# Two graph layers on one core: the first part of the row sums one piece sooner, and one addition of the first layer behind it

## The chip, the cores and the metric

The kernel runs on one core of a Trainium2 chip. The core has five engines with an instruction stream of their own: TensorE (PE) multiplies matrices and writes to the banks of PSUM; its weight loads are listed apart as PEld. VectorE (DVE), ScalarE (ACT) and GpSimd (POOL) work on tiles element by element, and SyncE (SP) issues the transfers (DMA). Each engine runs its instructions in the order of its stream; between engines, an instruction waits for a semaphore. The metric is the device time of one execution in microseconds, as the median of several runs.

## The reference

The input `x` holds 64 graphs with 256 nodes and 512 features, the adjacency matrix `adj` is common to all. There are two layers, each behind a layer norm and a ReLU, each added to its input:

```
h = relu(layernorm(x))
x = x + layer0(h, adj)          # graph attention, one head
h = relu(layernorm(x))
x = x + layer1(h, adj)          # masked attention, eight heads of 64
```

Layer 0 multiplies `h` with a weight of 512x256, forms one score per edge from two vectors, masks and normalises the scores, and puts the weighted sum of the neighbours beside the product itself. Layer 1 projects `h` to queries, keys and values (512x512 each), masks the scores with the same adjacency, normalises them over the neighbours, weighs the values and projects the result with a fourth 512x512 matrix. All is in 32-bit floating point.

## The kernel before

**Groups and phases.** The 64 graphs are taken in 32 groups of two. The main loop (line 1178) runs over the groups `g` and within each over its two graphs `b`. In group `g` the attention of layer 1 is done for the two graphs, and beside it, in pieces, the projections of group `g+1` (`project`), layer 0 of group `g+2` (`first_layer`) and the first layer norm of a later group (`first_norm`). Each of these is a Python generator; a call of `next` emits one piece of it into the instruction streams.

**The step strings.** Which piece follows which is written by hand in two strings (line 1176), one per graph. A letter is one piece: `S` the scores of all eight heads, `m` one masking, `u` a projection, `o` an output product of the graph before, `n` a norm, `s` a piece of layer 0, `f` a piece of `fold`, `v` the differences of the values. Group 0 has a string of its own for its first graph (line 1184), and so has the last group.

**Order on the engines.** TensorE is held to the order of emission by `in_order` (line 131): every matmul is made to follow the one emitted before it. The other engines' instructions are placed by a scheduler, which knows their data dependencies and estimated times; `not_sooner` (line 123) pins an instruction behind the last one that the same wrapper (`Remembers`, line 27) issued to its engine. All of the instructions that go through the wrapper appear under line 35 in the profile, and all matmuls under line 137.

**Seven products.** The big matrix products are done as seven half-size products with sums of blocks (a Strassen-Winograd scheme). For layer 0 this is `first_products` (line 636), from group 2 on. It has seven pieces, with two PSUM banks, `first` and `second`. In the order of emission these are product 1, 2, 6, 7, 5, 4 and 3. `first` accumulates products 1, 6, 5 and 3, `second` product 2 and then, in a new bank, 7 and 4. ScalarE copies a bank aside after products 1, 6 and 7 (`kept`). VectorE adds bank and copy into a quarter of `H` after product 2 (`part(0, 0)`), after product 5 (`part(1, 1)`) and after product 4 (`part(1, 0)`). ScalarE copies the last quarter after product 3. As the bank is read after product 5 and written again by product 3, product 3 waits for that addition. After product 4, `score_rows` (line 621) transposes a few columns of `H` and sends them through memory to all partitions, and GpSimd adds `H` to `x` for the residual. In the profile the seven appear as `ph`: product 6 as `ph<-w_more,sums_xn`, 7 and 4 as `ph<-w_more,hT`, 5 as `ph<-w_sb,sums_r`, and 3 as `ph<-w_sb,sums_xn`.

**Row sums.** The normalisation of layer 1 needs the sum of each row of the exponentials `p`. `fold` (line 984) makes it without TensorE, for every group but the last, in six pieces for two quads of four heads:

1. `put(0)` writes the first quad to memory, `fetch(0)` reads it back rearranged, as `parts` (one transfer and four);
2. `put(1)` writes the second quad;
3. GpSimd adds `parts` down in two additions (`add`, line 1009);
4. `sum_up(0)` (line 1013): VectorE transposes `parts` in blocks and reduces it to `compact`; then `fetch(1)` reads the second quad into the same buffer, with four transfers on SP, each pinned to SP's order;
5. the additions for the second quad;
6. `sum_up(1)` and a reciprocal, which `weigh` (line 1038) uses.

The buffer of `parts` of the first graph is also that of layer 0's edge scores `e`.

In the first string the seven pieces of layer 0 stand in `sssosfsfss`: the pieces of products 1, 2 and 6, an output product, product 7, piece 3 of `fold`, product 5, piece 4 of `fold`, and products 4 and 3.

Of the kernel before, what the change touches and what calls it, by code (L numbers as in the profile page):

```python
# [41 lines left out]
def two_gnn_layers(tc, *args):  # L42

    nc = tc.nc
    with tc.tile_pool(name="verdict", bufs=1) as pool:
        wrong = pool.tile([1, 1], I32, name="wrong")
        bounded(tc, *args, wrong)  # L50
        again = nc.values_load(wrong[0:1, 0:1], min_val=0, max_val=1)
        with tc.If(again > 0):
            tc.strict_bb_all_engine_barrier()
            any_inputs(tc, *args)
# [3 lines left out]
def bounded(  # L58
# [24 lines left out]
    vector, scalar, gpsimd, sync = (  # L83
        Remembers(e) for e in (nc.vector, nc.scalar, nc.gpsimd, nc.sync)
    )
# [23 lines left out]
    def mm(name):  # L109
        return psum.tile([P, 512], F32, tag="turn", name=name, bufs=5)  # L110
# [4 lines left out]
    def after(instruction, name):  # L115

        tc.add_manual_dep(
            instruction.ins, name,
            mybir.DependencyInfo(mybir.DependencyClass.NoSync, mybir.DependencyReason.DATA),
            reason="the engine's order",  # L120
        )

    def not_sooner(engine, operation, *args, **kwargs):

        last = engine.last
        after(getattr(engine, operation)(*args, **kwargs), last)
# [9 lines left out]
    def matmul(*args, **kwargs):  # L136
        in_order(nc.tensor.matmul(*args, **kwargs))  # L137
# [483 lines left out]
    def score_rows(g):  # L621
        rows = small.tile([P, GT, 8], F32, tag="rows", name=f"rows_{g}", bufs=2)
        last = vector.last
        turned = vector.transpose(rows.rearrange("p t c -> p (t c)"), H[:, :, 0:8])
        for other in [last, *fold_last] if g >= 2 else [last]:
            after(turned, other)
        line = dram.tile([P // 8, S], F32, tag="line", name=f"line_{g}")
        not_sooner(sync, "dma_start", line, rows.rearrange("p t c -> p (t c)")[::8, :])
        own = att.tile([P, P // S, GT, S], F32, tag="r", name=f"own_{g}", bufs=1)
        not_sooner(  # L630
            sync, "dma_start", own.rearrange("p k t j -> p (k t j)"),
            line.rearrange("(o k) j -> o (k j)", o=1).to_broadcast([P, TOK]),
        )
        return own.rearrange("p k t j -> p t k j")

    def first_products(g):
        ops = operands.pop(("first", g))
        forms = {
            1: w0_sb[:, :2, :FH], 2: w0_sb[:, 2:, :FH], 3: w0_sb[:, 2:, FH:], 5: w0_sb[:, :2, FH:],
            6: w0_more[:, 0], 7: w0_more[:, 1], 4: w0_more[:, 2],  # L640
        }

        def bank(name):
            return mm(f"ph{name}_{g}")[:, : NT * FH].rearrange("p (t o) -> p t o", t=NT)

        def product(out, i, start):
            a = ops[i]
            for t in range(NT):
                for c in range(2):
                    matmul(  # L650
                        out[:, t, :], a[:, c, t * P : (t + 1) * P], forms[i][:, c, :], start=start and t == c == 0,
                        stop=t == c == 1, skip_group_check=True,
                    )

        def part(b, half):
            return H[:, b * NT : (b + 1) * NT, half * FH : (half + 1) * FH]

        def kept(out, i):
            s = att.tile([P, 2, N], F32, tag="kept", name=f"kept{i}_h_{g}", bufs=3)
            s = s.rearrange("p t n -> p (t n)")[:, : NT * FH].rearrange("p (t o) -> p t o", t=NT)  # L660
            last = list(put_last)
            copied = scalar.copy(s, out)
            if i == 0:
                for other in last:
                    after(copied, other)
            return s

        def residual_from(b):
            xt = xs[g, b][:, :, F1:]
            not_sooner(gpsimd, "tensor_add", xt, H[:, b * NT : (b + 1) * NT, 2 : F1 + 2], xt)  # L670

        first = bank(1)
        product(first, 1, True)
        p1 = kept(first, 0)
        yield
        second = bank(2)
        product(second, 2, True)
        vector.tensor_add(part(0, 0), second, p1)
        yield
        product(first, 6, False)  # L680
        p16 = kept(first, 1)
        yield
        second = bank(7)
        product(second, 7, True)
        p7 = kept(second, 2)
        yield
        product(first, 5, False)
        vector.tensor_add(part(1, 1), first, p7)
        yield
        product(second, 4, False)  # L690
        vector.tensor_add(part(1, 0), second, p16)
        owns[g] = score_rows(g)
        residual_from(1)
        yield
        product(first, 3, False)
        scalar.copy(part(0, 1), first)
        residual_from(0)

    def first_layer(g):

        xt = [xs[g, b][:, t, :] for b in range(GB) for t in range(NT)]
        if g > 1:
            yield from first_products(g)
# [469 lines left out]
    additions = (piece for g in range(NG) for piece in residual(g))  # L1173


    steps = ("Smmnfuuuumonmnuofuusssosfsfssuvnofunonfosuo", "Ssmmfusmusmfuososfuosfrsuuonufrounfouunsous")
    waiting, late, folds = None, iter(()), iter(())
    for g in range(NG):
        products = project(g + 1) if g + 1 < NG else iter(())
# [423 lines left out]
```

## Time and profile before

| | us |
|---|---|
| median of three runs | 2392.16 |
| lowest and highest run | 2390.17, 2392.17 |
| time of the profiled execution | 2390.06 |
| its span, first to last instruction | 2388.3 |
| TensorE busy in the span | 2375.2 |
| VectorE busy | 1705.2 |
| GpSimd busy | 1430.5 |
| ScalarE busy | 1023.0 |

The mean granted clock of TensorE is 1.000 of full speed. A line of the timeline gives start and duration in microseconds, the engine, the line of the program, the operation, the tile written and the tiles read, the shape and the number of instructions merged into it; in brackets stands the idle time ahead and what ended it. A line of the waits gives the engine and tile that waited, the engine and tile waited for, the total in microseconds, the number of times and the longest. The chain follows the work that ended last back to the start.

A group takes some 73 us. The stretch from 247 to 255 us, in which layer 0's products of one group run, is like that in all other groups but the first and the last ones.

### The profile page before, as it was taken

Reading aid. Unit: us, or ns where it says so; the run is one execution under the profiler, and the core shown is the slowest. Engines: PE = TensorE matmul, PEld = TensorE weight load, DVE = VectorE, ACT = ScalarE, POOL = GpSimd, SP = SyncE. Lnnn points to the kernel's source line nnn. Section 1 sums busy time; section 2 is a strip of 40 time slices with the busy share of each in tenths; the row PEclk is TensorE's granted clock in tenths of the full one; section 3 lists DMA queues with packets and bytes.
Section 4 is the critical chain, followed back from the end, with each engine's and each line's share of the span. In section 5 each row is a group of like instructions: output and inputs, shape, how many; then the busy total and the mean of one; then the engine's idle time right before and its main releaser. Section 6 shows DMA issues by size and latency. Waiting matters only on the chain.

```text
span 2388.3 us, 43029 instructions
## 1 busy us (share of the span) xinstructions
PE 2375.2 (99%) x15828; PEld 1993.8 (83%) x15828; DVE 1705.2 (71%) x3345; ACT 1023.0 (43%) x2017; POOL 1430.5 (60%) x1290
## 2 busy tenths in 40 slices
PE   9999999999999999999999999999999999999998
PEld 8888888888888888888888888888888888888886
DVE  7578676686766777767777667776677676777666
ACT  5444444343443444444444434444444444343431
POOL 4565655755657555666656575566665565655552
PEclk9999999999999999999999999999999999999999
DMA  5444445454445544454444455444554445554331
GB/s 185 129 147 146 145 130 163 149 151 143 140 143 155 168 144 137 133 163 149 146 146 140 152 150 161 150 135 139 163 151 146 143 134 161 151 161 141 107 109 46
DMA packets 271864, 343.49 MB, mean 144 GB/s; under 512 B 25376, under 2 KB 217120, under 8 KB 271648
## 3 DMA queue, kind: packets, MB, share of 16 engines
q1 hardware_dynamic: 271648, 340.69, 46.6%
q8 instruction: 126, 2.06, 0.4%
q14 instruction: 90, 0.74, 0.1%
HBM read 176.95 MB, written 163.64 MB: 143 GB/s over the span
## 4 chain that ended last, share of the span: by engine, by line
PE 95%; DVE 2%; ACT 1%; issue 1%; DMA 0%; POOL 0%; SPq 0%; DVEq 0%; ACTq 0%; POOLq 0%
PE pq L137 16%; PE pv L137 16%; PE py L137 16%; PE pk L137 15%; PE sc L137 10%; PE pr L137 9%; PE ph L137 8%; PE po L137 4%; DVE p L35 1%; DMA a_b<-in_L_gnn_a_dram 0%; ACT xn L35 0%; DVE x L35 0%; DVE st L35 0%; ACT e L35 0%; PE total L137 0%
## 5 line engine op out<-in xcount | busy, mean ns | idle before, releaser
L35 POOL TENSOR_TENSOR p<-p 128x512 f32<-128x512 f32 x248 | 393.0, 1598 | 480.9 <-DVE p L35 477.1
L35 ACT ACTIVATE xn<-x,factor 128x512 f32<-128x512 f32 x256 | 194.8, 807 | 412.2 <-POOL factor L35 405.0
L35 DVE TENSOR_TENSOR p<-p,maskT 128x1024 f32<-128x1024 f32 x254 | 347.4, 1389 | 3.2 <-ACT p L35 3.2
L35 DVE TENSOR_TENSOR x<-py,x 128x256 f32<-128x256 f32 x448 | 184.6, 412 | 204.1 <-PE py L137 197.9
L35 ACT ACTIVATE p<-sc 128x512 f32<-128x512 f32 x512 | 257.7, 627 | 94.7 <-PE sc L137 78.3
L35 POOL TENSOR_TENSOR parts<-parts 128x512 f32<-128x512 f32 x248 | 248.1, 1000 | 67.9 <-DMA parts<-rows 54.5
L137 PE MATMUL py<-wo_sb,oT 128*128 128x256 f32 x1024 | 262.4, 379 | 0.6 <-DVE oT L35 0.6
L137 PE MATMUL pk<-hT,wk_sb 128*128 128x256 f32 x1024 | 244.8, 382 | 0.0
L137 PE MATMUL sc<-q,k 64*128 64x256 f32 x2048 | 241.9, 385 | 0.1
L137 PE MATMUL pq<-hT,wq_sb 128*128 128x256 f32 x1024 | 240.1, 382 | 1.1 <-ACT hT L35 0.7
L137 PE MATMUL pv<-wv_sb,hT 128*128 128x256 f32 x1024 | 236.8, 379 | 0.0
L137 PE MATMUL pr<-p,v 128*32 128x256 f32 x4096 | 234.2, 380 | 0.0
L137 PEld LDWEIGHTS sc<-q,k 64*128 64x128 f32 x2048 | 190.8, 187 | 51.8 <-issue 26.3
L35 POOL TENSOR_TENSOR factor<-factor,rexp 128x2 f32<-128x2 f32 (+1 forms) x132 | 117.8, 892 | 178.7 <-DVE factor L35 178.2
L137 PEld LDWEIGHTS pq<-hT,wq_sb 128*128 128x128 f32 x1024 | 191.8, 190 | 36.7 <-issue 10.3
L137 PEld LDWEIGHTS py<-wo_sb,oT 128*128 128x128 f32 x1024 | 194.2, 190 | 28.2 <-DVE oT L35 1.1
L137 PEld LDWEIGHTS pk<-hT,wk_sb 128*128 128x128 f32 x1024 | 189.7, 190 | 33.3 <-issue 9.9
L137 PEld LDWEIGHTS pv<-wv_sb,hT 128*128 128x128 f32 x1024 | 194.6, 190 | 26.5
L137 PEld LDWEIGHTS pr<-p,v 128*32 128x32 f32 x4096 | 126.8, 110 | 97.8 <-issue 18.6
L137 PE MATMUL py<-wo_sb,o_sums 128*128 128x256 f32 x768 | 197.6, 380 | 0.5 <-DVE x L35 0.5
L137 PE MATMUL pv<-wv_sb,sums 128*128 128x256 f32 x768 | 184.2, 383 | 1.9 <-ACT kept_v L35 1.9
L137 PE MATMUL pq<-sums,wq_sb 128*128 128x256 f32 x768 | 181.5, 379 | 0.0
(150 smaller groups left out, 4066.3 us busy)
## 6 DMA issues: line engine op xcount, KB each, us to landing
passed<-xt SPq DMA_DIRECT2D x124, 512.0 KB, 2.9
moved<-passed SPq DMA_DIRECT2D x496, 128.0 KB, 3.5
rows<-p SPq DMA_DIRECT2D x124, 512.0 KB, 3.4
parts<-rows SPq DMA_DIRECT2D x496, 128.0 KB, 3.0
x<-in_x_dram SPq DMA_DIRECT2D x64, 512.0 KB, 4.5
out_dram<-x SPq DMA_DIRECT2D x62, 512.0 KB, 4.0
own<-line SPq DMA_DIRECT2D x30, 256.0 KB, 3.2
wq_sb<-in_L_gnn_Wq_dram SPq DMA_DIRECT2D x2, 512.0 KB, 9.6
```

Of the source, the lines that this page charges most:

```text
L35: instruction = getattr(self.engine, operation)(*args, **kwargs)
L137: in_order(nc.tensor.matmul(*args, **kwargs))
```

## The change

Two edits. In the first string, `sfsf` becomes `sffs` with one `s` behind: piece 4 of `fold` (the transpose and reduction of the first quad and the four transfers that fetch the second) is now emitted before layer 0's piece with product 5, directly behind piece 3. And the addition of that piece, `part(1, 1)`, is pinned behind the last VectorE instruction, which is then the reduction of piece 4. For group 2 of layer 0, which runs beside main group 0 with its own string, the addition stays as it was.

```
@@ first_products
         product(first, 5, False)
-        vector.tensor_add(part(1, 1), first, p7)
+        if g == 2:
+            vector.tensor_add(part(1, 1), first, p7)
+        else:
+            not_sooner(vector, "tensor_add", part(1, 1), first, p7)
         yield
         product(second, 4, False)
         vector.tensor_add(part(1, 0), second, p16)
@@ the step strings
-    steps = ("Smmnfuuuumonmnuofuusssosfsfssuvnofunonfosuo", "Ssmmfusmusmfuososfuosfrsuuonufrounfouunsous")
+    steps = ("Smmnfuuuumonmnuofuusssosffsssuvnofunonfosuo", "Ssmmfusmusmfuososfuosfrsuuonufrounfouunsous")
```

## The prediction

> **What bounds the kernel now.** I read the share of busy time by engine first, then the chain that ended last, then the waits of the matmul engine, then the timeline of one of the places that the change touches.
>
> ```profile
> span 2388.3 us, 43029 instructions
> PE 2375.2 (99%) x15828; PEld 1993.8 (83%) x15828; DVE 1705.2 (71%) x3345; ACT 1023.0 (43%) x2017; POOL 1430.5 (60%) x1290
> ...
> PE 95%; DVE 2%; ACT 1%; issue 1%; DMA 0%; POOL 0%; SPq 0%; DVEq 0%; ACTq 0%; POOLq 0%
> ```
>
> TensorE is busy for 2375.2 of 2388.3 us and carries 95% of the chain. Its instructions run in the order in which the program emits them, so a wait of one matmul stops all that follow, and each microsecond of such a wait is a microsecond of the kernel. How much of that there is today, the waits of PE tell:
>
> ```profile
> PE pv L137 <- ACT kept_v L35: 1.9, 3, 1.1
> PE warm L137 <- POOL square_ones L35: 1.1, 1, 1.1
> ```
>
> Columns: total, times, longest. The whole table sums to 7.0 us, and most rows happen once, at the start or the end. So nothing can make this kernel faster by more than about 7 us, and a new wait of 1 us in each group would cost some 30 us. The timeline of the place, in one of the 32 groups (start, duration, engine, operation, tiles):
>
> ```profile
> 250.33 0.73 POOL L35 TENSOR_TENSOR parts<-parts 128x256 f32<-128x256 f32 x1
> ...
> 251.07 1.06 PE L137 MATMUL ph<-w_sb,sums_r 128*128 128x129 f32 x8
> ...
> 251.97 1.06 PE L137 MATMUL ph<-w_more,hT 128*128 128x129 f32 x8
> 252.24 0.43 DVE L35 TENSOR_TENSOR H<-ph,kept_h 128x258 f32<-128x258 f32 x1 [1.43 <-PE ph L137]
> ...
> 252.86 1.08 PE L137 MATMUL ph<-w_sb,sums_xn 128*128 128x129 f32 x8
> 253.06 0.43 DVE L35 TENSOR_TENSOR H<-ph,kept_h 128x258 f32<-128x258 f32 x1 [0.40 <-PE ph L137]
> 253.41 0.43 DVE L35 STREAM_TRANSPOSE parts<-parts 128x256 f32<-128x256 f32 x1
> ...
> 253.87 0.42 DVE L35 TENSOR_REDUCE compact<-parts 128x8 f32<-128x256 f32 x1
> ...
> 254.21 0.20 DVE L35 STREAM_TRANSPOSE rows<-H 128x32 f32<-128x32 f32 x1
> ```
>
> The three PE lines are the fifth, fourth and third product, back to back. The addition at 252.24 is the fifth product's: it reads the bank `first`, ends at 252.67, and 0.19 us later the third product begins to accumulate into that same bank. The addition at 253.06 is the fourth product's. Behind it, and only there, VectorE takes the transpose and reduction of the row sums, although GpSimd had finished their input at 251.06.
>
> **The change part by part.**
>
> *The new order on VectorE.* The source moves the row sums' transpose and reduction ahead of the piece with the fifth product, and pins that product's addition behind them. But in the order of instructions as built, which each engine keeps, the scheduler still places the transpose behind the fourth product's addition. The order is now: fourth product's addition, transpose, reduction, fifth product's addition. So the fifth product's addition is not merely behind the row sums, it is behind the fourth product as well. It is so in 29 groups (main groups 1 to 29). Group 0 has its own step string, group 30 has no first layer left to move past, and group 31 has no such sums. No instruction is added or removed, and TensorE's own order is unchanged.
>
> *The wait that this makes.* The third product overwrites the bank that the fifth product's addition reads, so it waits for it. By the timeline: the fourth product's addition starts at 253.06 as now, the transpose at 253.41, the reduction at 253.87, and the next VectorE instruction at 254.21. That place now belongs to the addition, with its 0.43 us, to 254.64. The same sequence already stands in group 0:
>
> ```profile
> 110.42 0.42 DVE L35 TENSOR_REDUCE compact<-parts 128x8 f32<-128x256 f32 x1
> 110.76 0.42 DVE L35 TENSOR_TENSOR H<-ph,kept_h 128x258 f32<-128x258 f32 x1
> ```
>
> There too the addition starts 0.34 us after the reduction. With the 0.19 us from the addition's end to the matmul, the third product starts at 254.83 instead of 252.86: 1.97 us later. TensorE has nothing else to run meanwhile. 29 x 1.97 = 57.1 us. Bounds: the third product shows no wait today, so perhaps the 0.19 is not all release time; a matmul that really waited, on a ScalarE copy that ended at 287.72, started at 287.77, and with 0.05 the delay is 1.83 (53.1 us). That same matmul took 0.48 against 0.38 for those behind it, so a restart may cost 0.10 more: 2.07 (60.0 us). I take 1.97, since the addition's end at 252.67 and the matmul's start are the nearest rows.
>
> VectorE's rows overlap: the transpose starts 0.35 us after an addition that lasts 0.43. [...] With full durations the addition would start at 253.06+0.43+0.43+0.42 = 254.34, 0.13 us later, and the sum would be 3.8 us larger. The trace decides for the smaller one.
>
> *What may be given back.* All other engines gain 1.97 us on TensorE in each of these groups. That can only remove waits which TensorE has. After the start-up there is the 1.9 us row above; I take that. Bounds: nothing, and 9.3 + 7.0 = 16.3 us, the two rows of weight loads that wait (for the copies `kept_v`, 27 times, and for the exponentials, 31 times) as if each stood on the path.
>
> *The fetch of the second part.* It is issued at 254.37 today, right behind the reduction. The reduction does not move in time, so neither do the four issues (0.43 us each); the small `line` transfer queued behind them on SP waits for the `rows` transpose and so goes 0.43 us later, behind the addition. Cost nothing: measured against TensorE all of it is some 1.5 us sooner.
>
> *Who else waits for the addition.* GpSimd's residual addition for the second batch starts at 253.57, behind the fourth product's addition; it needs both, so it starts at 254.68. It and the work queued behind it on GpSimd stay ahead of TensorE's 1.97. On GpSimd the two `factor` instructions now stand ahead of the other residual addition, which may wait 0.9 us for them; its row is first read some 15 us later.
>
> *Orders that shift elsewhere.* On ScalarE four score activations now stand between the two halves of one key copy. They end near 265.6 today and the copy's bank is next written at 272.5: 6 us of cover. In the second half of the group, one of the four fetches goes ahead of the `passed` transfer on SP (0.43 us), and VectorE takes an output addition and one statistic (0.42 + 0.66) ahead of two transposes. These lead to GpSimd's `sums`, done at 306.7 and read by TensorE at 310.0: 3.3 us of cover. Cost nothing; if the cover were gone, up to 1.1 us a group, 31 us.
>
> *Sum.* 57.1 - 1.9 = 55.2 us against the profiled execution's 2390.06 us (span 2388.3 and 1.8 around it): 2445.3. The median of the runs, 2392.16, lies 2.1 us above that execution, so 2447.
>
> **The rivals.**
>
> 1. *Not slower: the sums fit ahead of the fourth product's addition.* VectorE idles 1.43 us until 252.24 and the input is there at 251.06. Were transpose and reduction run then, they would end near 252.0 and the addition would start at 252.24 as now. It decides whether the transpose starts before about 251.45. Time: 2392, at best 7 us less, since no more PE wait is there to be won. Against it: the built order has them behind the fourth product's addition in all 29 groups, and VectorE does not reorder. 4%.
>
> 2. *More is given back*, up to the 16.3 us: 2433. For it: the load rows exist. Against: TensorE itself shows gaps at only three of those 27 places. 6%.
>
> 3. *A second wait comes on top:* the transpose waits for GpSimd, or the shifted orders of the second half lose their cover. Each microsecond in 29 groups is 29 us; the 31 us above give 2478. Against: GpSimd ends 2.35 us ahead of the transpose, and the other covers are 3.3 us and more. 6%.
>
> 4. *The clock falls in the new gaps.* The largest gap of today is 1.11 us, at 582 us, with a granted clock of 1.00 after it. At the end, the last matmul is over at 2382.7 and the clock holds for over 3 us:
>
> ```profile
> 2384.00:2386.00 2.00, 0.00 (x0) 0.00 (x0) 0.00 (x0) 0.00 (x0) 0.00 (x0) 1.00 0.25 81
> 2386.00:2388.30 2.30, 0.00 (x0) 0.00 (x0) 0.00 (x0) 0.00 (x0) 0.00 (x0) 0.66 0.04 11
> ```
>
> The third value from the right is the clock. A gap of 2 us is inside that. If each of the 29 were yet followed by a stretch like the last line, 2.30 us at 0.66, TensorE would lose 0.78 us in each, 23 us: 2470. I give it 2%. [...]
>
> **How the numbers follow.** The forecast holds 82%: 2447, with its own range from 53.1 us less a third of the 16.3 given back (2440) to 60.0 with nothing given back (2452). The range reaches a little into cases 2 and 3, to 2438 and 2455, and leaves out less than 2 in 10. Some 0.2% (5 us) is what a measurement of this kernel can tell from no change. Only case 1 ends within that or below: faster 0.01, same 0.03, slower 0.96.
>
> **What would show it.** In the changed profile: a row "PE ph waits for DVE H" with 29 entries of about 1.9 us; the additions at that place one behind the reduction; the third product some 2 us behind the fourth product's end; PE busy time as before and its share near 97%; the clock at 1.00. A PE row without such waits, or the transpose ahead of the fourth product's addition, would make me wrong; PE waits at `pv`, `pq` or `sc` longer than today would mean the size is.

## The result

The changed kernel takes 2442.05 us (median of six runs, 2440.22 to 2443.78), the kernel before 2391.16 us in runs beside it (2389.51 to 2392.25). The ratio is 1.0214, with a 95% interval of 1.0201 to 1.0227: 2.1% slower, 50.9 us. The forecast was 2447, with a range of 2438 to 2455.

The page of the changed kernel, first its span, busy times and chain:

```profile
span 2438.6 us, 43079 instructions
...
PE 2376.1 (97%) x15828; PEld 2001.0 (82%) x15828; DVE 1682.1 (69%) x3345; ACT 1013.4 (42%) x2017; POOL 1429.0 (59%) x1290
...
PE 95%; DVE 2%; issue 1%; POOL 1%; ACT 0%; DMA 0%; DVEq 0%; SPq 0%; ACTq 0%; POOLq 0%
```

TensorE is busy for 0.9 us more than before, in a span that is 50.3 us longer. So TensorE does no more work, it stands still. Where, its waits say (total, times, longest):

```profile
PE ph L137 <- DVE rows L35: 52.8, 29, 1.8
PE warm L137 <- POOL square_ones L35: 1.1, 1, 1.1
```

One row with 29 entries of 1.82 us carries all of it. And the timeline of the place, in the same group that the prediction showed:

```profile
254.30 0.43 DVE L35 TENSOR_TENSOR H<-ph,kept_h 128x258 f32<-128x258 f32 x1 [2.32 <-PE ph L137]
254.65 0.43 DVE L35 STREAM_TRANSPOSE parts<-parts 128x256 f32<-128x256 f32 x1
255.12 0.42 DVE L35 TENSOR_REDUCE compact<-parts 128x8 f32<-128x256 f32 x1
255.45 0.42 DVE L35 TENSOR_TENSOR H<-ph,kept_h 128x258 f32<-128x258 f32 x1
255.61 1.73 SPq L35 DMA_DIRECT2D parts<-rows  x4
255.79 0.20 DVE L35 STREAM_TRANSPOSE rows<-H 128x32 f32<-128x32 f32 x1
...
256.02 1.13 PE L137 MATMUL ph<-w_sb,sums_xn 128*128 128x129 f32 x8 [1.82 <-DVE rows L35]
```

The first line is the fourth product's addition, the one at 255.45 the fifth's. The third product starts at 256.02, 0.15 us behind that addition's end at 255.87. The profile names `rows` as what released it, since the little transpose ends at about the same time; the instruction that the third product needs is the addition at 255.45, which reads its bank.

The trace also shows a place that the prediction did not look at, some 10 us later in the group. Before the change (all lines of VectorE, but for the scores `sc` on TensorE):

```profile
262.61 0.42 DVE L35 TENSOR_TENSOR x<-py,x 128x256 f32<-128x256 f32 x1 [0.87 <-PE py L137]
...
263.42 0.42 DVE L35 TENSOR_REDUCE compact<-parts 128x8 f32<-128x256 f32 x1
...
266.10 3.81 PE L137 MATMUL sc<-q,k 64*128 64x256 f32 x32
...
267.08 1.29 DVE L35 TENSOR_TENSOR oT<-pr,r 128x512 f32<-128x512 f32 x2
```

And after it:

```profile
264.56 0.40 DVE L35 TENSOR_REDUCE compact<-parts 128x8 f32<-128x256 f32 x1
...
265.82 0.42 DVE L35 TENSOR_TENSOR x<-py,x 128x256 f32<-128x256 f32 x1 [0.58 <-PE py L137]
...
269.30 3.73 PE L137 MATMUL sc<-q,k 64*128 64x256 f32 x32
269.44 0.69 DVE L35 TENSOR_TENSOR oT<-pr,r 128x512 f32<-128x512 f32 x1 [0.22 <-PE pr L137]
```

Before, VectorE waits 0.87 us for TensorE's last output product, adds it to `x`, and only then takes the transpose and reduction of the second quad; `oT`, which needs these sums, ends 2.27 us behind the start of the scores. After, the sums come first and the waiting addition behind them, and `oT` (the line is the second of its two instructions) ends 0.83 us behind the start of the scores, which now take 3.73 instead of 3.81 us.

Laid side by side, with every TensorE segment counted from the start of the fifth product (median of 26 like groups), the two traces differ at four places only: the third product starts 1.98 us later; its restart costs 0.05; the scores `sc` give back 0.087; and the value products and the output product behind them 0.023 and 0.104. So 29 x 2.03 = 58.9 us are lost and 29 x 0.21 = 6.2 us given back. The spans differ by 50.3, so another 2.4 us come from places that are not in every group. Most of it comes from the three value products of the row `PE pv <- ACT kept_v` (1.9 us before): it is gone, and they start 0.55, 0.56 and 1.27 us sooner. Given back in all: 8.6 us.

### The profile page after: what moved, and what is told of

Read it like the earlier page. It is cut to its first block, busy times and chain, and to the rows that moved or that the text cites. A ratio compares the mean times of both kernels' runs of the same rounds, so it can differ in the third digit from the quotient of the medians.

```text
span 2438.6 us, 43079 instructions
## 1 busy us (share of the span) xinstructions
PE 2376.1 (97%) x15828; PEld 2001.0 (82%) x15828; DVE 1682.1 (69%) x3345; ACT 1013.4 (42%) x2017; POOL 1429.0 (59%) x1290
## 4 chain that ended last, share of the span: by engine, by line
PE 95%; DVE 2%; issue 1%; POOL 1%; ACT 0%; DMA 0%; DVEq 0%; SPq 0%; ACTq 0%; POOLq 0%
PE pq L137 16%; PE pk L137 16%; PE py L137 16%; PE pv L137 15%; PE sc L137 10%; PE pr L137 9%; PE ph L137 8%; PE po L137 4%; DVE parts L35 1%; DVE compact L35 1%; DVE H L35 1%; PE warm L137 0%; POOL parts L35 0%; ACT hT L35 0%; PE total L137 0%
## 5 line engine op out<-in xcount | busy, mean ns | idle before, releaser
L35 DVE TENSOR_TENSOR p<-p,maskT 128x1024 f32<-128x1024 f32 x254 | 327.0, 1308 | 3.2 <-ACT p L35 3.2
L137 PEld LDWEIGHTS sc<-q,k 64*128 64x128 f32 x2048 | 193.3, 187 | 46.5 <-issue 26.3
```

Source lines behind the costliest of these rows:

```text
L35: instruction = getattr(self.engine, operation)(*args, **kwargs)
```

## The experiments

Theory 1: the loss is the fifth addition's place behind the fourth's addition and the sums, and the third product waits for it. Rival: the loss comes with the earlier sums and fetch as such. What then was to be explained was the 8.6 us given back. All kernels were timed beside the kernel before on the same chip, which took 2389.9 to 2390.5 us there. A kernel with the pin alone was not run: the instruction lists of its build are those of the kernel before.

**e1: the string alone.** On the kernel before:

```
-steps = ("...sssosfsfss...
+steps = ("...sssosffsss...
```

> The new step string without the pin on the fifth product's addition. As built, the order on every engine is that of the kernel before. My theory (all of the loss is the place of the fifth product's addition behind the fourth product's on VectorE): 2391, within 0.2% of the kernel before, no wait of product 3 in the waits of TensorE. A rival in which the earlier fold itself costs or gains time by another way: several us off 2391.

Measured: 2390.16 us, ratio 1.0001 (0.9992 to 1.0010). With the string alone the scheduler places every instruction of every engine as before. The change has an effect only where both edits stand together: the pin forces the fifth addition behind the reduction, and the scheduler keeps the reduction behind the fourth addition.

**e3: the fourth product's addition behind the sums too.** On the changed kernel, pinned in the same way:

```
 product(second, 4, False)
-vector.tensor_add(part(1, 0), second, p16)
+if g == 2:
+    vector.tensor_add(part(1, 0), second, p16)
+else:
+    not_sooner(vector, "tensor_add", part(1, 0), second, p16)
```

VectorE's order is then transpose, reduction, fifth addition, fourth addition; the sums run in the idle time ahead of both.

> The changed kernel with the fourth product's addition also pinned, behind the fifth's, so that VectorE takes transpose, reduction, fifth's addition, fourth's addition. My theory: the transpose then runs in VectorE's idle time from about 251.1 of the group shown, the fifth's addition starts at 252.2 as in the kernel before, TensorE does not wait, and the time is 2391 (2386 to 2394); the fetch is issued some 2.3 us sooner and buys nothing, since TensorE waits for none of it. Rival (the sums ahead of product 5's addition cost TensorE a wait in any order): 2400 to 2442. Rival (the earlier fetch was worth something that the wait hid): 2380 to 2386.

Measured: 2383.92 us, ratio 0.9973 (0.9963 to 0.9984). Its timeline at the place:

```profile
251.95 0.45 DVE L35 STREAM_TRANSPOSE parts<-parts 128x256 f32<-128x256 f32 x1 [0.40 <-POOL parts L35]
252.43 0.42 DVE L35 TENSOR_REDUCE compact<-parts 128x8 f32<-128x256 f32 x1
...
252.98 0.43 DVE L35 TENSOR_TENSOR H<-ph,kept_h 128x258 f32<-128x258 f32 x1
...
253.60 1.08 PE L137 MATMUL ph<-w_sb,sums_xn 128*128 128x129 f32 x8
```

The fifth addition starts 1.16 us behind the start of its product, as in the kernel before, so the sums do not delay it; it ends 0.19 us ahead of the third product, which waits in no regular group (one wait of 1.0 us in the whole kernel). That is all of the 58.9 us, so theory 1 stands: the earlier sums cost nothing where VectorE takes them in time. But the kernel also beats the one before, by 6 us. That lies in the range of the second rival, that the earlier fetch is worth something; e6 and e9 test where it comes from. The trace shows the same small gains at the same three places as the changed kernel (0.086, 0.022 and 0.104 us a group). On its page, the busy times:

```profile
PE 2370.0 (99%) x15828; PEld 1998.8 (84%) x15828; DVE 1693.1 (71%) x3345; ACT 1017.1 (43%) x2017; POOL 1424.3 (60%) x1290
```

TensorE's busy time is 5.2 us shorter than before, with as many matmuls, and only 0.9 us of the 6.1 by which the span shrinks are idle time. So "busy" holds short waits too: here those of the weight loads within the scores and the value products, whose rows were 7.0 and 9.3 us before and are at most 1.0 here.

**e5: TensorE late, the order around the second quad's sums as before.** The question was whether the 8.6 us came back simply because all other engines had 2 us more. On the kernel before, nine idle products of 128x128 ones into unused columns of the bank `first` were put ahead of the third product:

```
+        if g > 2:
+            for _ in range(9):
+                matmul(banks["first"][:, 384:512], square_ones, square_ones, start=False, stop=False, skip_group_check=True)
```

> The kernel before with nine matmuls of 128x128 ones into unused columns of the bank ahead of product 3 in the same 29 groups: TensorE is some 2.0 us later there (the changed kernel: 2.03), and the order of all other engines stays that of the kernel before. Of the 58.9 us of the changed kernel's wait about 8 are given back later in the groups. Theory A (the others catch up while TensorE stands, whatever the order): the nine matmuls cost 58 us and 6 to 9 are given back, 2440 to 2443; weight loads wait for kept_v and for the exponentials no more. Theory B (the shifted orders behind the sums gave it back): nothing or at most 2 us given back, 2447 to 2450, and both rows of waits stay at 9.3 and 7.0 us.

Measured: 2448.41 us, 58.5 over the kernel before. Its weight loads wait as before:

```profile
PEld pv L137 <- ACT kept_v L35: 9.7, 27, 1.5
PEld sc L137 <- ACT p L35: 7.0, 31, 0.5
```

Both rows were 9.3 and 7.0 and are 0.2 and 0.5 in the changed kernel. Here they stay, and nothing is given back: TensorE is 1.99 us later from the third product on, and ScalarE's copy `kept_v` 1.98 us (median of the same groups). So the work that TensorE feeds came late with it. The orders are not quite those of the kernel before: on VectorE one output addition of each group moved behind the statistics that stood after it, as it did in the changed kernel too. What was given back comes from another order.

**e6: the last output addition behind the sums.** On the kernel before, this one addition of a group's second graph is made to follow the reduction of the second quad; on no other engine does an instruction change its place:

```
-        add(0, 1, first)
+        made = add(0, 1, first)
+        if b == 1 and g < NG - 2:
+            after(made, fold_last[0])
```

> The kernel before, in which only the last output addition of a group's second graph (it waits for TensorE's late output product) is placed behind the transpose and reduction of the second quad of sums instead of ahead of them; everything else keeps its place, product 5's addition too. Theory i (what was given back in the changed kernel comes from the sums no longer standing behind that addition): the rows for kept_v (9.3 us) and ACT p (7.0 us) vanish, the period goes from 73.19 to about 72.98 us, and the time is 2384 us (2382 to 2387). Theory ii (it comes from the shifts on the second graph's side, which this kernel does not make): 2390 us (2388 to 2392), both rows stay.

Measured: 2384.62 us, ratio 0.9979 (0.9970 to 0.9988). In its timeline:

```profile
261.50 0.42 DVE L35 TENSOR_REDUCE compact<-parts 128x8 f32<-128x256 f32 x1
261.99 0.42 DVE L35 TENSOR_TENSOR x<-py,x 128x256 f32<-128x256 f32 x1
...
265.16 1.29 DVE L35 TENSOR_TENSOR oT<-pr,r 128x512 f32<-128x512 f32 x2
...
265.47 3.81 PE L137 MATMUL sc<-q,k 64*128 64x256 f32 x32
```

`oT` now starts ahead of the scores, not 0.98 us behind their start. The gains at the value and output products are there (0.023 and 0.104), the `kept_v` row is all but gone (0.2 us), and the span is 6.0 us shorter. So this exchange alone gives 6 us, the `kept_v` part of what was given back. Counted from the start of the fifth product, `oT` ends 1.29 us sooner than before, and `kept_v`, 18 us further on, starts 1.29 us sooner. The other part, 0.087 us at the scores, does not come with it: the scores still take 3.81 us and the row for `p` keeps its 7.0 us. By the instruction lists, the fifth of these score products waits for ScalarE before the change and in e6, and for VectorE in the changed kernel and in e3: it has been given another bank.

**e8 and e9: the exchange undone.** On the changed kernel (e8) and on e3 (e9), the last piece of `fold` is emitted at the end of the string:

```
-steps = ("...unofunonfosuo", ...
+steps = ("...unofunonosuof", ...
```

VectorE then takes the last output addition ahead of the second quad's transpose again. ScalarE's two key copies, which the change had split, go back together with it.

> The changed kernel, in which the last output addition of a group's second graph stands ahead of the transpose and reduction of the second quad of sums again, as before the change; ScalarE's two key copies stand together again with it, and the order ahead of product 3 is the changed kernel's. Theory i (the 8.6 us that were given back in the changed kernel come from the sums going ahead of that addition): the 1.8 us waits ahead of product 3 stay and nothing is given back, 2442 + 6 to 8.6, so 2448 to 2451 us; the rows for kept_v and ACT p come back. Theory ii (they are given back elsewhere, such as by the other shifts or by the shorter work of VectorE in the gap): 2442 us, within 2 us.

> The kernel in which both additions of the first layer stand behind the first quad's sums (2383.9 us, 6 us under the kernel before), with the last output addition ahead of the second quad's sums again. Theory i: with it goes the whole gain, 2390 to 2392 us, so that the first quad's earlier sums and the earlier fetch have bought nothing. Theory ii: the earlier sums and fetch of the first quad are worth something by themselves, 2384 to 2388 us.

Measured: e8 2458.85 us (2458.34 to 2459.19), 16.8 over the changed kernel; e9 2402.75 us (2402.14 to 2405.14), 18.8 over e3 and 12 over the kernel before, ratio 1.0052 (1.0039 to 1.0066). Both miss both theories: I expected 6 to 9 us to be lost, and 17 to 19 were. Nor did the old rows come back, as the expectation for e8 had it: in e8 `kept_v` stands at 1.7 us and `p` at 0.9. From e8, first the row of its waits that is new, then its timeline:

```profile
PEld sc L137 <- DVE oT L35: 8.8, 29, 0.3
```

```profile
266.42 0.42 DVE L35 TENSOR_TENSOR x<-py,x 128x256 f32<-128x256 f32 x1 [1.51 <-PE py L137]
...
267.23 0.42 DVE L35 TENSOR_REDUCE compact<-parts 128x8 f32<-128x256 f32 x1
...
269.91 4.33 PE L137 MATMUL sc<-q,k 64*128 64x256 f32 x32
...
270.90 1.29 DVE L35 TENSOR_TENSOR oT<-pr,r 128x512 f32<-128x512 f32 x2
```

The scores take 4.33 instead of 3.73 us, and they wait for `oT`: 0.60 us in each of 29 groups, 17.3 us, which is nearly all of the loss. So the changed kernel holds two things in that place. Its score products were given a bank that VectorE reads for `oT`; where `oT` is early, that is better than the bank that ScalarE reads for `p` (0.087 us a group), and where it is late, it is worse (0.51, so 0.60 between the two). And VectorE's exchange makes it early. In the changed kernel the 32 weight loads of the scores run through in 3.32 us, so their second half, in which the wait lies, begins some 1.6 us behind their start, at about 270.9; `oT` ends at 270.13, some 0.8 us earlier. In e8 the second half would begin at about 271.5, and `oT` ends at 272.19, over 0.6 us too late.

e9 against the kernel before answers the question that e3 left: TensorE's segments agree to 0.015 us from the fifth product on until these scores. In the group at 252 us the first quad's transpose starts 0.43 us behind the start of TensorE's fifth product instead of 2.34, and the reduction and the fetch behind it are as much earlier; it buys nothing there. Behind the scores, `oT` and `kept_v` keep the times of the kernel before to 0.005 us, while TensorE is 0.51 us later. So the value and output products still gain 0.02 and 0.105 us in e9. This gain does not need the exchange; here it comes because TensorE reaches them 0.51 us later and the work for them does not.

Why the scores are given another bank is left open. It is not the split key copies: in e8 and e9 these stand together and the bank is still the new one. The four kernels with another order ahead of product 3 have it (the changed one, e3, e8, e9); e6, which keeps that order, has the old one.

**e4 and e7: a longer wait.** The prediction held that the clock would not fall in gaps of 2 us. To see what a longer gap does, the first quad's reduction of the changed kernel was made twice (e4) and three times (e7) in the 29 groups, which writes the same sums again:

```
+for _ in range(2 if quad == b == 0 < g else 0):   # e7; e4 has one
+    not_sooner(
+        vector, "reduce_sum",
+        compact[:, quad], parts[:, 1].rearrange("p (k a) -> p k a", a=S), axis=AX.X
+    )
```

> The changed kernel with the reduction of the first quad made twice in the 29 groups (the same sums written again), one more VectorE instruction of 0.42 us ahead of the fifth product's addition. My theory (what stands on VectorE between the fourth product's end and that addition is on the path in full): 0.34 to 0.46 us in each of 29 groups, 10 to 13 us over the changed kernel: 2452 to 2455; the gap ahead of product 3 grows from 1.82 to about 2.2 us. Rival (the gap comes from a fixed latency or another wait): no more than 3 us over it.

> The changed kernel with the first quad's reduction made three times over in the 29 groups (the same sums are written again). Each repeat has cost 0.45 us of the wait ahead of product 3, so the gap is 2.73 us and the waits cost 13 us more than with two reductions. Theory A (the clock falls once a gap is long enough, somewhere between 1.82 and 2.73 us, and 2.27 us was at the edge): the clock falls to half behind nearly all 29 gaps, 1.7 us each, 49 us instead of 12: about 2517 us (2505 to 2525). Theory B (whether it falls depends on something beside the gap's length, so that about as many gaps are hit as before): 2480 us, up to 2492.

Measured: e4 2466.89 us, 24.8 over the changed kernel and some 12 more than expected; e7 2492.83 us, 50.8 over it, just past the upper end of theory B. The third product's gap grows by 0.453 us with each reduction, to 2.27 and 2.73 us. That is 13.1 and 26.3 us, about half of the loss. The rest is the clock, which fell to 0.5 for 3.41 us behind 7 of the 29 gaps of e4 and behind 14 of those of e7 (the mean granted clock is 0.995 and 0.990). Theory A, that it falls behind nearly all in e7, is out; theory B is right that something beside the length decides, but expected as many falls as in e4. Half of that time is 1.705 us for each fall: 7 x 1.705 = 11.9, 14 x 1.705 = 23.9, and the sums are 25.0 and 50.2, where 24.8 and 50.8 were measured. Behind the 29 gaps of 1.82 us in the changed kernel it never fell: its mean is 1.000.

Two gaps of one length can differ in this. In e7, one fall starts at 335.39 us and another 153.60 us later, which is 45 times 3.4133, the length of a fall. Laid out in stretches of that length from 335.39 us on, and back from it, these are two gaps of e7, each 2.73 us long (columns: stretch and its length; busy time of PE, PEld, DVE, ACT and POOL; granted clock, DMA share, GB/s):

```profile
331.98:335.39 3.41, 0.71 (x6) 0.74 (x7) 3.19 (x10) 0.00 (x0) 0.78 (x1) 1.00 0.00 1
335.39:338.80 3.41, 3.41 (x11) 2.82 (x11) 1.05 (x5) 0.38 (x1) 2.60 (x5) 0.50 0.59 154
338.80:342.21 3.41, 3.41 (x17) 2.98 (x16) 0.72 (x2) 2.24 (x4) 3.01 (x3) 1.00 0.20 77
```

```profile
407.07:410.48 3.41, 2.48 (x23) 2.29 (x21) 1.05 (x4) 0.38 (x1) 0.28 (x1) 1.00 0.00 0
410.48:413.90 3.42, 1.62 (x12) 1.57 (x13) 3.25 (x10) 0.38 (x1) 1.18 (x1) 1.00 0.20 58
413.90:417.31 3.41, 3.41 (x17) 3.02 (x16) 0.64 (x3) 2.07 (x4) 3.11 (x4) 1.00 0.39 97
```

The first gap lies within one stretch, which is idle for 2.70 us, and the clock is at 0.50 for the whole next one. The second is cut by an edge into 0.93 and 1.80 us, and the clock stays at 1.00. My estimate from these two is that the fall depends on how much of a gap lies in one such stretch. How much it takes is, as an estimate from the counts above, between 1.82 us, behind which none of 29 gaps had a fall, and 2.27 us, behind which 7 of 29 had one.

## Why the prediction was right, point by point

- **The new order on VectorE:** right, in 29 groups, by the timeline above.
- **The wait that this makes:** 57.1 us forecast (53.1 to 60.0), 58.9 measured. The third product starts 1.98 us later, where 1.97 was forecast; the restart, of which the upper bound spoke (0.10), cost 0.05. That the 1.97 fits so closely is in part luck: the fourth product's addition starts 0.07 us later against TensorE than before, and the release takes 0.15 instead of 0.19.
- **VectorE's overlapping starts:** the overlap seen in the trace, and not full durations, gave the right start. The fifth addition starts 0.33 us behind the start of a reduction that lasts 0.42.
- **What may be given back:** this is the mis-sized term. I took 1.9 us and 8.6 came, within the bounds of 0 to 16.3. That is 6.7 us too little; as the wait was 1.8 us larger than forecast, the sum is off by 5. The reason given was wrong too: "All other engines gain 1.97 us" gives nothing back, as e5 shows. It came from the step that I had put down as costing nothing, the orders that shift elsewhere.
- **Orders that shift elsewhere:** I looked for cover at `sums` and at one key copy, and the place that matters was neither. Moving the last output addition behind the second quad's sums is worth 6 us by itself (e6). Together with the new bank of the scores it makes the difference between a gain of 0.087 and a loss of 0.51 us a group (e8, e9). That the shifts came out as a gain was luck with some 0.8 us to spare.
- **The fetch of the second part:** worth nothing, as forecast; e9 shows it, where the sums and the fetch behind them are 1.9 us sooner against TensorE and nothing comes of it up to the scores.
- **Rival 1, the sums ahead of both additions:** didn't occur, and e3 shows that its mechanism is real: with that order the wait is gone, and the kernel ends 6 us below the one before. The rival's most of 7 us was read wrongly all the same: it is the sum of TensorE's listed waits, and 5.2 of the 6.1 us by which the span of e3 shrinks come out of its busy time. The 16.3 us of weight loads that wait stood outside that sum.
- **Rival 4, the clock:** the clock stayed at 1.00, and the forecast was right with too little margin. "A gap of 2 us is inside that" was argued from the end of the kernel, where the clock holds for over 3 us. By e4 and e7 that argument fails: behind gaps of 2.27 us the clock fell 7 times in 29, behind gaps of 2.73 us 14 times. The gap was 1.82. At that end the clock fell at 2386.72; the 3.41 us ahead of this, from 2383.31, are idle as a whole, and in the 3.42 us ahead of those TensorE is busy for 2.84, so only 0.6 us are idle there.
- **What would show it:** the row has 29 entries of 1.8 us as forecast, but names `rows` and not `H`.

## What to carry to other kernels

Before moving work ahead of an instruction that another engine waits for, look where the scheduler has put the neighbours: a pin behind work that is itself queued behind a later instruction puts all of it ahead of the one that is waited for. On an engine that keeps its order, as VectorE does in these traces (in the changed kernel the addition at 255.45 stands behind the reduction at 255.12), an instruction that waits should stand behind work that is ready; that exchange alone, on this kernel's VectorE, is worth 6 us. And a changed emission order also changes which banks are handed out, so that a harmless shift can set up a wait that only another shift hides.

## What the runs showed of the hardware

The granted clock of TensorE fell to 0.5 for 3.41 us behind 7 of the 29 gaps of 2.27 us in e4 and behind 14 of the 29 gaps of 2.73 us in e7; behind the 29 gaps of 1.82 us in the changed kernel it did not fall. The price was 1.7 us for each fall, half of the 3.41. So the same gap of 2.73 us cost nothing more in 15 groups and 1.7 us more in 14; the two that are shown above differ in how the stretches of 3.41 us divide them.
